# Retention and cross attention of a decoder layer: two stages run one after the other, and the same work issued in one interleaved order

## The chip, the cores and the metric

The kernel runs on one core of a Trainium2 chip. The core has five engines that run their own instruction queues in order: TensorE (PE in the profile; PEld is its weight load), VectorE (DVE), ScalarE (ACT), GpSimd (POOL) and SyncE (SP, which here only issues DMAs). Matmuls write to PSUM, of which there are eight banks of 128 partitions by 512 fp32 values; the other data lie in SBUF. The metric is the time of one execution on the device in microseconds: the median of the runs. All arithmetic here is fp32, except one bf16 matmul that is named below.

## The reference

Input `x` has 16 batches of 128 positions by 512 features; three sublayers follow, each with a residual and a LayerNorm.

1. **Retention**, 16 heads of width 32. For each batch `Q`, `K`, `V`, `G` are projections of `x` (four 512x512 weights). `Q` and `K` are rotated (`x*c + rot(x)*s`, neighbours swapped in pairs). `ret = (Q K^T) * D` with a decay matrix `D`, `Y = ret V`; `Y` is normalised within each head (mean and variance over 32 values), scaled and shifted; the result is `(G * sigmoid(G) * Yn) @ W_O`, added to `x` and normalised.
2. **Cross attention over the feature axis**: the 512 features are the sequence, the 128 positions the channels; 8 heads of width 16. Scores are kept only in a band `|i - j| <= 64`; outside it the softmax weight is zero. Output projection, `relu`, multiplication by `ctx_2048[n]`, a last 128x128 projection, residual, LayerNorm.
3. **A selected feed-forward block**: the 16 best positions of each batch (by a router score) go through an attention block and a gated MLP, and are written back; all other positions only get the last LayerNorm.

## The kernel before

The kernel has three stages, one after the other.

**Retention** (lines 113 to 317) works on `G = 8` groups `g` of two batches. The weights are loaded once; `load(g)` fetches the transposed group `xT` and its rows `xg`. The steps of a group are functions: `rotated` (16 matmuls in the record into one bank; DVE swaps pairs with a stream shuffle and multiplies with the cosine, POOL multiplies the swapped half with the sine and adds), twice for q and twice for k; `values` (once for each batch); `gates` (twice; ACT applies Silu, L206); `retain` (twice: scores of 8 heads into four banks, multiplied by the decay on DVE, L223); `weigh` (twice: times V; ACT writes the square and a copy, L246 and L247); `variance` (a matmul that averages the squares; ACT takes the root, L104, DVE the reciprocal, L105); `normalise` (spreads the factor back over four banks; eight DVE instructions, L269 and L271); `finish` (once for each batch: output projection; DVE adds the row and takes its moments; after both batches, POOL computes the inverse root in one chain, L289 and L290, and DVE writes the normalised rows `xr[n]`, L292). A loop issues the projections of group `g`, the middle steps of group `g - 1` and the `finish` of group `g - 2`, all from one pool of eight PSUM banks and working tiles of two buffers.

**Cross attention** (lines 343 to 574) works on units `m = 0..31`, two for each batch (`n = m // 2`, four heads each). `project` makes q and k of a unit (ACT moves them out of PSUM with the bias, L407), `project_v` the values of a batch. `scores(m, half)` computes half a unit's banded scores in four banks, and DVE adds the band and takes each row's maximum (L435, eight instructions). `lower(m)` transposes the maxima and subtracts them from q (L448). `weights(m, half)` computes the transposed scores: first one bf16 matmul for each of the four banks writes the band itself, an identity times a tile with 0 inside and a huge negative value outside (L457), then the score matmuls add to it (L462), and ACT takes the exponential (L467). `attend(m)` multiplies with the values, `divide(m)` transposes and normalises; `turn(n)` and `project_out(n)` make the output (ACT relu, then POOL times `enc`, L510), and `settle(n)` does the last projection (L516) and the LayerNorm: DVE moments, a chain of four small POOL instructions (L524 to L529), DVE writes `xr[n]` (L530) and the router score (L532), ACT writes the copy `z_plain` (L536), which SP stores.

The order of issue is written out by hand, and each engine runs its part of it in order. For one unit `m` it is: `scores(m+1, 0)`, `project` q, in even units `settle(n-2)`, `weights(m, 0)`, `attend(m-1)`, `project` k, `scores(m+1, 1)`, `divide(m-1)`, in even units `project_v`, `weights(m, 1)`, in odd units `turn(n-1)`, `lower(m+1)`, in odd units `project_out(n-1)`. PSUM is divided into six banks for `scores` and `weights` (a call takes four of them) and two, called misc here, that all other steps take in turn.

Between the two stages all buffers of the first are given back, six 1 MB weight parts of the feed-forward stage are loaded (L331), then the small weights of cross attention (L357).

**The feed-forward stage** follows; the change does not touch its instructions.

## Time and profile before

| what | value |
|---|---|
| median of three runs | 1154.94 us (1154.24 to 1155.27) |
| the profiled execution: its own time | 1148.59 us |
| its span | 1146.8 us |
| first retention matmul | 10.55 us |
| end of the last retention matmul | 353.8 us |
| first cross matmul / first `scores` | 379.33 / 385.90 us |
| last cross work (router score), start of selection | 862.2 us |
| end | 1146.8 us |
| one retention group in the steady part | 41.08 us (start of `normalise`'s matmuls at 70.19 and at 111.27) |
| one cross batch in the steady part | 28.56 us (`project_v` at 452.11 and at 480.67) |

How to read the profile: its first part gives the busy time of each engine. A view in stretches gives, for each stretch of the span, the busy time of PE, PEld, DVE, ACT and POOL with the number of instructions, then the granted TensorE clock (1.00 is full), the share of the DMA engines and their GB/s. The timeline lists instructions in order of time: start, duration, engine, line, what is written from what, and in brackets how long the engine had been idle and who ended that. The groups list, for equal instructions, the busy time, the mean duration in ns, and the idle time before them. Matmul durations in groups overlap each other; what a matmul group costs PE is better read from the distance of the next group's start in the timeline.

### The profile page before, as it was taken

To read this page: it belongs to the slowest core of one execution; us is meant where nothing else is said; L and a number is where in the kernel's file an instruction comes from. 1 tells how busy PE (TensorE), PEld (TensorE's weight loads), DVE (VectorE), ACT (ScalarE), POOL (GpSimd) and SP (SyncE) were. 2 spreads that over 40 slices of the span, in tenths; PEclk is the share of its full clock that TensorE was granted. 3 is DMA by queue.
4 is the path that set the end of the run, shared out by engine and by line. 5 is a ranking of instruction groups with operands and counts; after the bars stand their busy time and mean duration, and the time that the engine had idled before them with its cause. 6 is when DMAs were issued, how large, how long until landed. Compare 5 with 4: busy or idle time off the path is not lost.

```text
span 1146.8 us, 17444 instructions
## 1 busy us (share of the span) xinstructions
PE 990.1 (86%) x6987; PEld 611.4 (53%) x6987; DVE 502.8 (44%) x1778; ACT 338.6 (30%) x660; POOL 170.5 (15%) x189
## 2 busy tenths in 40 slices
PE   6999999999973699999999999999850898788995
PEld 5766767676641355555555555555420574445862
DVE  3344544453552355555555555555424344621102
ACT  0122012112120254444444444444420432411110
POOL 3312312322301001111111111111113141000000
PEclk9999999999996699999999999999965899999998
DMA  9110110010004400000000000000002143004410
GB/s 321 38 37 1 38 37 17 22 37 1 1 1 165 139 1 11 20 19 20 20 20 20 20 20 20 20 20 20 29 9 73 37 139 118 1 1 147 147 37 18
DMA packets 27600, 53.39 MB, mean 47 GB/s; under 512 B 3824, under 2 KB 4608, under 8 KB 27264
## 3 DMA queue, kind: packets, MB, share of 16 engines
q1 hardware_dynamic: 25296, 50.69, 13.3%
q10 hardware_dynamic: 2064, 1.07, 0.4%
q8 instruction: 55, 0.90, 0.3%
q0 software_dynamic: 160, 0.52, 0.1%
q14 instruction: 25, 0.20, 0.1%
HBM read 47.55 MB, written 4.73 MB: 46 GB/s over the span
## 4 chain that ended last, share of the span: by engine, by line
PE 30%; issue 19%; DVE 8%; ACT 7%; POOL 3%; DMA 2%; SPq 1%; POOLq 0%; DVEq 0%
PE xs_ps L427 5%; ACT xp_t L467 5%; PE xt_ps L462 4%; PE qk_ps L702 4%; PE xqk_ps L406 4%; DVE x_masked L435 3%; PE xt_ps L457 3%; PE xav_ps L476 2%; PE xout_ps L507 2%; PE xv_ps L412 1%; DVE bn_st L109 1%; PE xut_ps L489 1%; POOL rs L527 1%; DVE h L518 1%; PE xmx_ps L446 1%
## 5 line engine op out<-in xcount | busy, mean ns | idle before, releaser
L435 DVE CUSTOM_DVE_ANT_0 x_masked<-xs_ps,x_band 128x192 f32<-128x192 f32 (+1 forms) x512 | 164.7, 387 | 142.5 <-PE xs_ps L427 142.1
L467 ACT ACTIVATE xp_t<-xt_ps 128x448 f32<-128x448 f32 x256 | 118.1, 547 | 85.9 <-PE xt_ps L462 85.9
L427 PE MATMUL xs_ps<-xkT,xqT 32*128 32x256 f32 (+1 forms) x1024 | 92.3, 385 | 3.4 <-ACT xp_t L467 1.4
L427 PEld LDWEIGHTS xs_ps<-xkT,xqT 32*128 32x128 f32 x1024 | 58.4, 185 | 51.8 <-issue 36.6
L510 POOL TENSOR_TENSOR xy<-xy,enc 128x512 f32<-128x512 f32 x16 | 20.3, 1267 | 397.9 <-ACT xy L509 397.9
L188 POOL TENSOR_TENSOR swapped<-swapped,consts 128x512 f32<-128x512 f32 x32 | 40.6, 1268 | 206.0 <-DVE swapped L184 205.0
L180 PE MATMUL qT_ps<-xT,w_W_Q 128*128 128x256 f32 x256 | 60.5, 391 | 10.6 <-DMA xT<-in_xT 10.6
L462 PE MATMUL xt_ps<-x_qa,xkT 32*128 32x192 f32 (+1 forms) x1024 | 67.3, 377 | 0.1
L457 PE MATMUL xt_ps<-band_b,ident_b 128*128 128x448 bf16 x256 | 62.2, 356 | 3.7 <-DVE x_mx L435 3.7
L246 ACT ACTIVATE sq<-y_ps 128x512 f32<-128x512 f32 x16 | 9.6, 597 | 174.8 <-PE y_ps L241 174.8
L282 PE MATMUL o_ps<-w_W_O,y 128*128 128x512 f32 x128 | 59.8, 613 | 1.1 <-DVE y L271 1.1
L462 PEld LDWEIGHTS xt_ps<-x_qa,xkT 32*128 32x128 f32 x1024 | 44.0, 186 | 31.2 <-issue 29.8
L406 PE MATMUL xqk_ps<-xp,x_w_q 128*128 128x512 f32 x64 | 37.9, 676 | 25.5 <-DMA x_w_v<-in_w_v 25.5
L180 PE MATMUL kT_ps<-xT,w_W_K 128*128 128x256 f32 x256 | 59.2, 385 | 0.0
L180 PEld LDWEIGHTS qT_ps<-xT,w_W_Q 128*128 128x128 f32 x256 | 49.3, 195 | 18.2 <-DMA xT<-in_xT 10.6
L194 PE MATMUL v_ps<-w_W_V,xT 128*128 128x512 f32 x128 | 58.8, 604 | 0.0
L203 PE MATMUL g_ps<-xT,w_W_G 128*128 128x256 f32 x256 | 58.4, 382 | 0.0
L476 PE MATMUL xav_ps<-xp_t,x_va 128*32 128x192 f32 (+1 forms) x1024 | 55.8, 359 | 0.0
L203 PEld LDWEIGHTS g_ps<-xT,w_W_G 128*128 128x128 f32 x256 | 48.1, 190 | 12.0 <-issue 6.1
L180 PEld LDWEIGHTS kT_ps<-xT,w_W_K 128*128 128x128 f32 x256 | 47.5, 190 | 8.1 <-issue 1.4
L407 ACT ACTIVATE xqT<-xqk_ps,x_b_q 128x512 f32<-128x512 f32 x32 | 22.0, 687 | 89.4 <-PE xqk_ps L406 89.4
L476 PEld LDWEIGHTS xav_ps<-xp_t,x_va 128*32 128x32 f32 x1024 | 30.3, 111 | 25.3 <-issue 12.2
(192 smaller groups left out, 1485.2 us busy)
## 6 DMA issues: line engine op xcount, KB each, us to landing
xT<-in_xT SPq DMA_DIRECT2D x8, 512.0 KB, 3.9
xg<-in_x SPq DMA_DIRECT2D x8, 512.0 KB, 4.8
wq<-in_wq SPq DMA_DIRECT2D x4, 1024.0 KB, 10.8
enc<-in_ctx SPq DMA_DIRECT2D x16, 256.0 KB, 2.8
out<-z_plain SPq DMA_DIRECT2D x16, 256.0 KB, 3.0
wo<-in_wo SPq DMA_DIRECT2D x4, 1024.0 KB, 5.3
w_gate<-in_w_gate SPq DMA_DIRECT2D x4, 1024.0 KB, 5.1
w_up<-in_w_up SPq DMA_DIRECT2D x4, 1024.0 KB, 5.1
```

The source lines that it names most:

```text
L180: nc.tensor.matmul(ps[:, i * GT:(i + 1) * GT], w[wname][:, kc, hg * P:(hg + 1) * P], st["xT"][:, kc, :], start=(kc == 0), stop=(kc == KC - 1))
L194: nc.tensor.matmul(ps, state[g]["xT"][:, kc, b * S:(b + 1) * S], w["W_V"][:, kc, :], start=(kc == 0), stop=(kc == KC - 1))
L203: nc.tensor.matmul(ps[:, i * GT:(i + 1) * GT], w["W_G"][:, kc, hg * P:(hg + 1) * P], state[g]["xT"][:, kc, :], start=(kc == 0), stop=(kc = ...
L282: nc.tensor.matmul(ps, st["y"][:, kc, b * S:(b + 1) * S], w["W_O"][:, kc, :], start=(kc == 0), stop=(kc == KC - 1))
L406: nc.tensor.matmul(ps, w[:, hg * P:(hg + 1) * P], xr[n], start=True, stop=True)
L427: nc.tensor.matmul(ps[j][:, OFF[c]:OFF[c] + LEN[c]], st["qT"][hs, hg, c * P:(c + 1) * P], st["kT"][hs, hg, LO[c]:LO[c] + LEN[c]], start=Tr ...
L435: nc.vector.tensor_tensor_reduce(out=junk[:, 0:LEN[c]], in0=ps[j][:, OFF[c]:OFF[c] + LEN[c]], in1=band[:, SEEN[c]:SEEN[c] + LEN[c]], scale ...
L457: nc.tensor.matmul(ps[j][:, 0:448], ident_b, band_b[:, half, :], start=True, stop=True)
L462: nc.tensor.matmul(ps[j][:, OFF[c]:OFF[c] + LEN[c]], kT[hs, hg, c * P:(c + 1) * P], qa[hs, LO[c]:LO[c] + LEN[c]], start=False, stop=True, ...
L467: nc.scalar.activation(p[:, half, j, :], ps[j][:, 0:448], AF.Exp, scale=XD ** -0.5)
L476: nc.tensor.matmul(ps[32 * j:32 * (j + 1), LO[c]:LO[c] + LEN[c]], va[:, c, hg * 4 + j, :], p[:, c // 2, j, OFF[c]:OFF[c] + LEN[c]], start= ...
L702: nc.tensor.matmul(ps[:, i * R:(i + 1) * R], w[(h0 + i) // 4][:, kc, at:at + P], hT[:, kc, :], start=(kc == 0), stop=(kc == KC - 1))
```

## The change

The two stages become one function `layers` with one order of issue.

- A loop runs `m` from -8 to 35. Each iteration issues the cross attention's steps of unit `m` in the old order, and between them up to four slots of retention steps that `plan(m)` lists. Four iterations (two batches of cross attention) carry one retention group, `g = m // 4 + 2`; `finish` writes rows two batches ahead of their use. Iterations -8 to -3 hold retention alone, 26 to 35 cross attention alone.
- PSUM: all steps share the cross attention's six plus two banks. `retain` and `normalise` take four of the six; `rotated`, `values`, `gates`, `weigh`, `variance` and `finish` take the two misc banks.
- The band: the bf16 matmuls (L457) are gone. `weights` takes the exponential of all columns, and then GpSimd sets what lies outside the band to zero with four `affine_select` instructions for each half unit, each on four heads by 128 (or 64) columns of the weights.
- The gate: ACT's Silu becomes `tanh(g/2)`, and DVE computes `(tanh + 1) * g`; the factor one half is put into `gn_weight` and `gn_bias`, which DVE multiplies by 0.5 at the start.
- Rows: `load` fetches the rows straight into `xr`, `finish` works on them in place, and each batch has its own inverse root on POOL.
- Working tiles of retention have one buffer instead of two in most places; the weights' tile `xp_t` has three half-unit buffers.
- Small weights of cross attention are loaded during retention; `decay` is loaded before `W_G`. Centring `W_V` on DVE is issued at the end of iteration -8. The six feed-forward weight parts are loaded at the end of iteration 25, when the retention buffers are given back.

```diff
+    def layers(left: ExitStack, right: ExitStack):
         G = B // GB
+        wp = right.enter_context(tc.tile_pool(name="ret_w", bufs=1, side="right"))
+        wk = right.enter_context(tc.tile_pool(name="ret_wk", bufs=1, side="right"))
+        xw = left.enter_context(tc.tile_pool(name="x_w", bufs=1))
+        xk = left.enter_context(tc.tile_pool(name="x_wk", bufs=2))
+        sp = left.enter_context(tc.tile_pool(name="scores_ps", bufs=6, space=PSUM))
+        mp = left.enter_context(tc.tile_pool(name="misc_ps", bufs=2, space=PSUM))
+
+        def score_bank(name):
+            return sp.tile([P, 512], F32, tag="score", name=name)
+
+        def misc_bank(name):
+            return mp.tile([P, 512], F32, tag="misc", name=name)
...
-            xT = wk.tile([P, KC, GT], F32, name="xT")
+            xT = wk.tile([P, KC, GT], F32, name="xT", bufs=2)
             nc.sync.dma_start(out=xT, in_=t["xT"][:, g])
-            xg = wk.tile([P, GB, D], F32, name="xg", bufs=4)
-            nc.sync.dma_start(
-                out=xg, in_=t["x"][g * GB:(g + 1) * GB].rearrange("b s d -> s b d"))
-            state[g] = dict(
-                xT=xT, xg=xg,
-                qT=wk.tile([P, 4, GB, S], F32, name="qT"),
-                kT=wk.tile([P, 4, GB, S], F32, name="kT"),
-                v=wk.tile([P, GB, D], F32, name="v"),
-                gate=wk.tile([P, 4, GT], F32, name="gate"))
+            for i in range(GB):
+                nc.sync.dma_start(out=xr[g * GB + i], in_=t["x"][g * GB + i])
+            state[g] = dict(xT=xT)
...
+            nc.vector.tensor_scalar_mul(v, v, 0.5)
...
+        def centre():
+
+            wv = w["W_V"].rearrange("p k (h d) -> p (k h) d", d=HD)
+            wmean = wp.tile([P, KC * NH], F32, name="w_mean")
+            nc.vector.tensor_reduce(wmean, wv, AX.X, ALU.add)
+            nc.vector.tensor_scalar_mul(wmean, wmean, 1.0 / HD)
+            nc.vector.tensor_tensor(wv, wv, bc(wmean, 2, HD), ALU.subtract)
...
-            nc.scalar.activation(state[g]["gate"][:, 2 * hp:2 * hp + 2, :],
-                                 ps.rearrange("p (i n) -> p i n", i=2), AF.Silu)
+            if hp == 0:
+                state[g]["gate"] = wk.tile([P, 4, GT], F32, name="gate")
+            pv = ps.rearrange("p (i n) -> p i n", i=2)
+            gt = state[g]["gate"][:, 2 * hp:2 * hp + 2, :]
+            nc.scalar.activation(gt, pv, AF.Tanh, scale=0.5)
+            nc.vector.scalar_tensor_tensor(gt, gt, 1.0, pv, ALU.add, ALU.mult)
...
+            sc = [score_bank(f"ret_ps{j}") for j in range(4)]
...
+            ps = [score_bank(f"spread_ps{hg}") for hg in range(4)]
...
-            if b == 0:
-                st["h"] = wk.tile([P, GB, D], F32, name="h1")
-                st["mv"] = small.tile([P, GB, 2], F32, name="mv1")
-            h, mv = st["h"], st["mv"]
-            ps = bank("o_ps")
+            row = xr[g * GB + b]
+            ps = misc_bank("o_ps")
             for kc in range(KC):
                 nc.tensor.matmul(ps, st["y"][:, kc, b * S:(b + 1) * S], w["W_O"][:, kc, :],
                                  start=(kc == 0), stop=(kc == KC - 1))
-            nc.vector.tensor_tensor(h[:, b, :], ps, st["xg"][:, b, :], ALU.add)
-            moments(mv[:, b, :], h[:, b, :])
-            if b < GB - 1:
-                return
-            rs = small.tile([P, GB], F32, name="rs1")
-            nc.gpsimd.tensor_scalar(rs, mv[:, :, 1], 1.0, EPS, ALU.mult, ALU.add)
-            nc.gpsimd.tensor_tensor(rs, rs, power, ALU.pow)
...
+            nc.vector.tensor_tensor(row, ps, row, ALU.add)
+            mv = small.tile([P, 2], F32, name="mv1")
+            moments(mv, row)
+            rs = small.tile([P, 1], F32, name="rs1")
+            nc.gpsimd.tensor_scalar(rs, mv[:, 1:2], 1.0, EPS, ALU.mult, ALU.add)
+            nc.gpsimd.tensor_tensor(rs, rs, power[:, 0:1], ALU.pow)
+            nc.vector.tensor_scalar(row, row, mv[:, 0:1], rs, ALU.subtract, ALU.mult)
+            if b == GB - 1:
+                state.pop(g)
...
             ps = [score_bank(f"xt_ps{j}") for j in range(4)]
-            for j in range(4):
-                nc.tensor.matmul(ps[j][:, 0:448], ident_b, band_b[:, half, :],
-                                 start=True, stop=True)
             for c in (2 * half, 2 * half + 1):
                 for j in range(4):
                     hs = slice(32 * j, 32 * (j + 1))
                     nc.tensor.matmul(ps[j][:, OFF[c]:OFF[c] + LEN[c]],
-                                     kT[hs, hg, c * P:(c + 1) * P],
+                                     kT[hs, c * P:(c + 1) * P],
                                      qa[hs, LO[c]:LO[c] + LEN[c]],
-                                     start=False, stop=True, skip_group_check=True)
+                                     start=True, stop=True)
             for j in range(4):
-                nc.scalar.activation(p[:, half, j, :], ps[j][:, 0:448], AF.Exp,
-                                     scale=XD ** -0.5)
+                nc.scalar.activation(p[:, j, :], ps[j][:, 0:448], AF.Exp, scale=XD ** -0.5)
+
+            for c in (2 * half, 2 * half + 1):
+                for sign, a, b in ((1, SEEN[c], P), (-1, P, SEEN[c] + LEN[c])):
+                    v = p[:, :, OFF[c] + a - SEEN[c]:OFF[c] + b - SEEN[c]]
+                    nc.gpsimd.affine_select(
+                        out=v, in_=v, pattern=[[0, 4], [sign, b - a]],
+                        base=a if sign == 1 else P - a, channel_multiplier=-sign,
+                        compare_op=ALU.is_ge, fill=0.0)
...
+        def ret(*units):
+            for f, g, *args in units:
+                if 0 <= g < G:
+                    f(g, *args)
+
+        def plan(m):
+
+            k, it = divmod(m, 4)
+            g = k + 2
+            if it == 0:
+                return ([(load, g + 1), (rotated, g, "q", "W_Q", 0, 0)], [(normalise, g - 1)],
+                        [(rotated, g, "k", "W_K", 1, 0)], [])
+            if it == 1:
+                return ([(finish, g - 1, 0)], [(retain, g, 0)],
+                        [(values, g, 0)], [(finish, g - 1, 1)])
+            if it == 2:
+                return ([(values, g, 1)], [(weigh, g, 0)],
+                        [(rotated, g, "q", "W_Q", 0, 1)], [(rotated, g, "k", "W_K", 1, 1)])
+            return ([(gates, g, 0)], [(retain, g, 1)],
+                    [(gates, g, 1)], [(weigh, g, 1), (variance, g)])
+
+        for m in range(-8, M + 4):
+            n, odd = divmod(m, 2)
+            nxt = 0 <= n + 1 < B
+            a, b, c, d = plan(m)
+            guarded(scores, m + 1, 0)
+            ret(*a)
+            if m == -6:
+                prepare()
+            if nxt:
+                project(n + 1, w_q, b_q, "q", odd)
+            if not odd and 0 <= n - 2 < B:
+                settle(n - 2)
+            guarded(weights, m, 0)
+            ret(*b)
+            guarded(attend, m - 1)
+            if nxt:
+                project(n + 1, w_k, b_k, "k", odd)
+            guarded(scores, m + 1, 1)
+            ret(*c)
+            if m == -8:
+                centre()
+            guarded(divide, m - 1)
+            if not odd and nxt:
+                project_v(n + 1)
+            guarded(weights, m, 1)
+            if odd and 0 <= n - 1 < B:
+                turn(n - 1)
+            ret(*d)
+            guarded(lower, m + 1)
+            if odd and 0 <= n - 1 < B:
+                project_out(n - 1)
+            if odd and 0 <= n < B:
+                encoder(n)
+            if m == 4 * (G - 1) - 3:
+                right.close()
+                start_ff()
+
+    first = {}
+
+    def start_ff():
+        nonlocal wff
+        wff = ctx.enter_context(tc.tile_pool(name="ff_w", bufs=7, side="right"))
+        first["wq"] = [kc_part("wq", i) for i in range(4)]
+        first["wk"] = [kc_part("wk", i) for i in range(2)]
+
+    with ExitStack() as left, ExitStack() as right, tc.manual_schedule():
+        layers(left, right)
```

## The prediction

> **What bounds the kernel now.** I read the page first, then stretches, then the timeline of one cross batch. Each stretch line gives the window, then PE, PEld, DVE, ACT and POOL busy, the granted clock, the DMA share and GB/s.
>
> ```profile
> span 1146.8 us, 17444 instructions
> 116.00:154.00 38.00, 38.00 (x260) 25.17 (x259) 16.69 (x31) 6.84 (x11) 11.02 (x10) 1.00 0.09 28
> 358.00:380.00 22.00, 0.67 (x1) 0.50 (x2) 0.00 (x0) 0.00 (x0) 2.74 (x6) 0.50 0.93 319
> 485.70:514.30 28.60, 26.51 (x249) 14.57 (x249) 15.70 (x77) 13.54 (x26) 2.88 (x5) 1.00 0.07 19
> ...
> 379.33 2.05 PE L406 MATMUL xqk_ps<-xp,x_w_q 128*128 128x512 f32 x2 [25.54 <-DMA x_w_v<-in_w_v]
> ```
>
> Retention is PE alone, with no idle time. Between the stages PE waits 25.54 us for weights. In cross attention every engine has idle time: there a chain sets the pace, and the next view shows which.
>
> ```profile
> 561.27 0.70 POOL L527 TENSOR_TENSOR rs<-rs,power 128x2 f32<-128x2 f32 x1
> 562.07 0.53 POOL L529 TENSOR_SCALAR shift<-mv,rs 128x1 f32<-128x1 f32 x1
> 562.63 0.81 ACT L536 ACTIVATE z_plain<-h,shift,rs 128x512 f32<-128x512 f32 x1 [4.40 <-POOL shift L529]
> 563.10 2.28 PE L427 MATMUL xs_ps<-xkT,xqT 32*128 32x256 f32 x16
> 563.35 1.82 ACT L467 ACTIVATE xp_t<-xt_ps 128x448 f32<-128x448 f32 x4
> ...
> 836.61 1.61 PE L507 MATMUL xout_ps<-xoT,x_w_outT 128*128 128x512 f32 x2 [1.91 <-ACT xoT L502]
> 840.35 2.07 PE L516 MATMUL xct_ps<-xy,x_w_ct 128*128 128x512 f32 x2 [2.12 <-POOL xy L510]
> ```
>
> The reader is to see two things. ACT works in order: `z_plain` waits for `settle`'s POOL chain, and the exponentials of `weights`, ready 2.8 us before, stand behind it; `scores` takes 2.28 instead of 1.0 us, because its banks wait for them. And after waits of about 2 us a matmul pair takes 2.07 us against 1.13 in the steady part (557.61): TensorE runs at half speed.
>
> **How I cost the new order.** I walk one period of four iterations, instruction by instruction, through the four in-order queues as the built kernel has them, with start-to-start distances of this profile. PE: `scores`, `weights` 0.97, `project` 1.05, `attend` 1.65, one `rotated` 3.46, `values` 3.43, `gates` 3.46, one `finish` 3.52, `retain` 1.11, `weigh` 1.01, `variance` 0.57, the four-transpose steps 0.59. DVE: eight maxima 2.55, a `rotated` 1.3, `normalise` 3.7, four decays 2.5. ACT: four exponentials 1.85. The same walk through the old even unit puts `attend`, `divide` and `project_v` within 0.3 us of the trace.
>
> PE's sum without the band is 18.4, 22.0, 22.2 and 20.1 us for iterations 4k to 4k+3: 82.7, and 83.7 with the 1.0 by which a measured group (41.08) exceeds its parts (40.1). Before, the same work takes 41.08 + 2 x 28.56 = 98.2. Waits that the walk finds:
> - 4k+3, 3.7 us: `retain` waits 1.0 for banks that exponentials hold; `turn` 0.75 for `divide`, behind the gate's new multiply on DVE; `variance` 1.0 for the square, behind four exponentials on ACT; `project_out` 1.1 for the misc bank that the root (table load 1.28, root 0.47) holds.
> - 4k, 7.4 us. From its first `scores`: `rotated` runs 1.4 to 4.9 (behind `lower`'s bank, as DVE subtracts only after the reciprocal of 1.75), DVE empties its bank by 6.5, `settle` runs 6.5 to 7.6, `weights` to 8.5, and its exponentials could begin at 8.7. But DVE's moments end at 9.3, POOL's chain at 11.1, `z_plain` at 12.0, and a table load (1.28, since the root came before) at 13.3: only then do they begin. `normalise` does two of its banks by 8.9 and needs the first exponential for another, at 13.75: PE idles 4.9. `attend` starts at 14.5, `scores` ends at 18.2, `rotated` k at 21.6, its bank is empty at 23.2, so `project_v` waits 1.0; the unit ends at 25.8. Other places 1.5.
> - 4k+1, 1.4 us: `retain` 0.9 for banks, the rest small.
> - 4k+2, 6.0 us: `values` waits 1.3 for `lower`'s bank, since DVE's subtraction stands behind `finish`, which waits for POOL; `project` k waits 3.9 for `weigh`'s bank, whose two reads on ACT stand behind the exponentials, behind `z_plain`; `project_v` 0.9.
>
> Sum 83.7 + 18.5 = 102.2. The waits of 4.9 and 3.9 exceed those after which the trace shows half speed; an episode lasts 3.3 us there (823.3 to 826.6) and so costs half, 1.7. I add two, and half of a third for the three waits near 1 us in 4k+3 (before 823.3, two of 1.2 within 8 us were enough): 4.2. The period is 106.4, between 102.2 (no episode) and 107.3 (three).
>
> [...]
>
> **Parts that the period holds, or that other work hides.**
> - Band: 256 bf16 matmuls, four in 0.85 us: 54 us of PE go, already left out. In cross attention alone the chain stays: by the walk an even unit takes 13.55 and an odd one 14.05, against 14.28 each.
> - Selections: 256, seven sizes of 512 elements for each unit in sum. No row has the operation. Bounds for one of 512: a memset 523 ns (L386), a two-input add 1385 (L189). I take 0.84, from the one-input copy (L650: 284 ns for 128) and the one-element memset (about 100): 100 + 512 x 1.44. A half unit takes 2.9; POOL is then busy about 41 of 106 us. At 0.52 the end is 2 us earlier; at 1.39, 13 later (`finish`'s POOL step stands behind them on POOL, as does `xy`, 1.1 a period and 6 at the end). A gain beyond that is excluded: they replace nothing on POOL.
> - Tanh: 16 DVE multiplies of 0.75 (as L518), and 8 Silu loads of 1.28 go; the loads left, for the root and back, are counted above.
> - Rows in place, an inverse root for each batch: one more POOL pair of 0.9 per group, inside the waits counted.
> - DMAs: `xT` of the next group stands on SP behind `enc`, which waits for POOL's `xy` early in iteration 4k; it is read a period later. The 25.54 us wait goes, since SP issues the small weights during retention, behind `W_O`. Six weight parts, 9.3 us of SP (357.76 to 367.08), come at iteration 25; behind them stand `z_plain` stores whose buffer is next written a batch later. The 105 us of cross units after it cover them; without that cover they cost their 20 us again. DVE's two multiplies by 0.5 wait for small loads that landed by 9.3, before its first eviction at 16.3: nothing.
>
> **Sum to the end of cross attention (862.2 before).** Iterations -8 to -1 hold two groups with little to fill in: the walk gives 103.7 (PE idles 3.5 for POOL's rotation at 19.5, 2.0 for the centring of `W_V`, one half-clock episode). Then 6 x 106.4 = 638.4, less 15.6 in the first period (no `settle`, `attend`, `turn` yet), 39 for iterations 24 and 25, and 105 for the rest (106.8 before from 755.4; 4 saved, one episode back). 103.7 + 638.4 - 15.6 + 39 + 105 = 870.5: 8.3 us later. The rest, 284.6, is unchanged. The profiled execution took 1148.59 us, 6.4 below the median of 1154.94; 8.3 on top gives 1156.9 and, at the median, **1163**. Less than 0.2% (2.3 us) is no change that this kernel's runs can tell.
>
> **The rivals.** Break-even is at a period of (862.2 - 232.1) / 6 = 105.0.
> - *Faster: the clock stays full.* If TensorE holds speed through the two long waits the period is 102.2 and the end 25 us earlier, 1138. For it: cross units keep clock 1.00 with waits of 1.2 each. Against: 836 to 842. It decides when fewer than two episodes fall in a period. Chance 0.27.
> - *The `z_plain` wait does not bite*, so PE stays near its sum: period 93 to 84, 1083 to 1029. Against: the built order has `z_plain`, the table load, then the exponentials. 0.06.
> - *Slow selections.* At 2 us each, `finish` and the last units lose 35 us: 1200; from 3.0 POOL's own sum (28 selections and 18 us of other work) passes the walked period. 0.17.
> - That the interleaving is not built as written is excluded by the built order.
>
> [...]
>
> **How the numbers follow.** The forecast holds 0.50 (1150 to 1178; slower 0.43, same 0.05, faster 0.02). The full-clock case gives faster 0.26, same 0.01; the third rival 0.06 faster; slow selections 0.17 slower. Together: faster 0.34, same 0.06, slower 0.60. The range 1120 to 1205 leaves out the third rival with the edge of the second's side, and the selections above 2 us.
>
> **What would show it.** After: `normalise`'s and `project` k's idle time put down to ACT's exponentials; clock below 1.00 between 110 and 730; a four-iteration period near 106; selections near 0.84; no wait for the small weights; `scoreT` near 870. A period below 105.0, or selections above 1.4, makes the forecast wrong.

## The result, and the profile after

The changed kernel takes 1171.9 us (median of four, 1170.2 to 1172.3) against 1154.6 us before: a ratio of 1.0157, with a 95% interval of 1.0126 to 1.0188. The sign of the forecast (1163, +0.7%) was right, its size less than half of what was measured. The profiled execution took 1170.15 us, 1.7 below its median; that of before stood 6.0 below the median of 1154.6. On the two profiles' own scale the change costs 21.6 us, where the working had 8.3.

First the page of the changed kernel: the span, two of the costliest groups, and the granted clock in tenths over 40 slices of the span.

```profile
span 1168.4 us, 17280 instructions
...
PEclk9999999899899989998998999888865799999998
...
L397 DVE CUSTOM_DVE_ANT_0 x_masked<-xs_ps,x_band 128x192 f32<-128x192 f32 (+1 forms) x512 | 199.7, 390 | 136.7 <-PE xs_ps L389 98.8
L433 POOL TENSOR_SCALAR_AFFINE_SELECT xp_t<-xp_t 128x512 f32<-128x512 f32 (+1 forms) x256 | 141.0, 588 | 268.2 <-ACT xp_t L428 268.2
```

The clock falls below 0.9 in five slices of the merged stage (those that begin at 204, 292, 409, 526 and 613 us), as foretold, and in every slice from 730 to 935 us, from just before cross attention runs alone until into the selection. Then the stretches of one period of four iterations (the first four lines, 4k to 4k+3, each from its first `scores` to the next) and of an odd and an even unit of cross attention alone. Columns: window, length, then PE, PEld, DVE, ACT and POOL busy with their counts, the granted clock, DMA share, GB/s.

```profile
407.82:436.78 28.96, 22.81 (x159) 14.28 (x158) 17.37 (x56) 7.68 (x13) 10.32 (x13) 0.88 0.16 56
436.78:460.63 23.85, 23.04 (x172) 12.35 (x171) 13.92 (x46) 8.18 (x17) 7.38 (x15) 1.00 0.00 1
460.63:489.46 28.83, 23.96 (x192) 15.91 (x191) 13.50 (x47) 9.08 (x17) 10.35 (x17) 0.94 0.06 20
489.46:513.46 24.00, 21.58 (x220) 14.65 (x219) 13.39 (x44) 10.16 (x18) 7.01 (x11) 1.00 0.00 1
786.78:800.62 13.84, 12.48 (x116) 6.92 (x115) 8.35 (x36) 7.36 (x15) 5.92 (x11) 1.00 0.35 129
800.62:817.72 17.10, 14.92 (x120) 9.23 (x119) 9.76 (x40) 6.10 (x12) 5.69 (x11) 0.80 0.10 32
```

The period is 105.6 us here (105.8 on average from one `variance` to the next, 298.03 to 721.13 in four), where 106.4 was forecast. Iterations 4k and 4k+2, which hold a `settle`, are 5 us longer than the others and are the ones with a clock below 1.00. In cross attention alone an odd unit takes 13.84, near its forecast; an even one takes 17.10 at a clock of 0.80, where 13.55 was forecast, and that is where the forecast fails.

The timeline of iteration 4k (start, length, engine, line, operation; in brackets the idle time before it and who ended it) shows the mechanism in the merged stage:

```profile
415.98 0.60 PE L330 MATMUL spread_ps<-gn_rs,spread 32*128 32x256 f32 x4
...
418.91 0.81 ACT L506 ACTIVATE z_plain<-h,shift,rs 128x512 f32<-128x512 f32 x1 [4.82 <-POOL shift L499]
...
419.74 1.28 ACT L428 ACT_TABLE_LOAD   x1
...
420.01 0.69 PE L330 MATMUL spread_ps<-gn_rs,spread 32*128 32x256 f32 x2 [3.43 <-DVE y L334]
...
421.03 1.85 ACT L428 ACTIVATE xp_t<-xt_ps 128x448 f32<-128x448 f32 x4
...
421.63 1.22 PE L330 MATMUL spread_ps<-gn_rs,spread 32*128 32x256 f32 x2 [0.93 <-ACT xp_t L428]
422.78 3.21 PE L444 MATMUL xav_ps<-xp_t,x_va 128*32 128x192 f32 x32
...
425.92 2.08 PE L362 MATMUL xqk_ps<-xp,x_w_k 128*128 128x512 f32 x2
```

`z_plain` waits for POOL, and the table load (ACT_TABLE_LOAD, 1.28 us; the trace has seven at this line, each between a root and the next exponentials) and the exponentials stand behind it. `normalise` waits 3.43 and 0.93 us, and then `attend` takes 3.21 us (1.72 at full speed) and `project` k 2.08 (1.13). Summed over the kernel, these waits (engine and line, who ended them, us, times, longest) are new or have grown:

```profile
PE spread_ps L330 <- DVE y L334: 21.1, 6, 3.9
PE xqk_ps L362 <- ACT y L312: 19.6, 6, 3.9
...
PE xs_ps L389 <- ACT xp_t L428: 7.6, 3, 3.1
```

The third line belongs to the even units at the end: three waits of 2 to 3 us for exponentials, where the sum had units without them. What makes them longer than before can be seen when the maxima of `scores` are laid side by side. Before, on DVE, in cross attention:

```profile
557.09 0.35 DVE L435 CUSTOM_DVE_ANT_0 x_masked<-xs_ps,x_band 128x192 f32<-128x192 f32 x1
557.37 0.08 DVE L435 DVE_READ_ACCUMULATOR2_ANT x_mx<- 128x1 f32 x1
557.37 0.42 DVE L435 CUSTOM_DVE_ANT_0 x_masked<-xs_ps,x_band 128x256 f32<-128x256 f32 x1
557.71 0.08 DVE L435 DVE_READ_ACCUMULATOR2_ANT x_mx<- 128x1 f32 x1
557.71 0.35 DVE L435 CUSTOM_DVE_ANT_0 x_masked<-xs_ps,x_band 128x192 f32<-128x192 f32 x1
```

After, in the even unit of the table above:

```profile
801.68 0.36 DVE L397 CUSTOM_DVE_ANT_0 x_masked<-xs_ps,x_band 128x192 f32<-128x192 f32 x1 [1.31 <-PE xs_ps L389]
801.96 0.08 DVE L397 DVE_READ_ACCUMULATOR2_ANT x_mx<- 128x1 f32 x1
802.08 0.42 DVE L397 CUSTOM_DVE_ANT_0 x_masked<-xs_ps,x_band 128x256 f32<-128x256 f32 x1
802.43 0.08 DVE L397 DVE_READ_ACCUMULATOR2_ANT x_mx<- 128x1 f32 x1
802.65 0.36 DVE L397 CUSTOM_DVE_ANT_0 x_masked<-xs_ps,x_band 128x192 f32<-128x192 f32 x1
...
805.35 0.75 DVE L488 SCALAR_TENSOR_TENSOR h<-xct_ps,x_b_ct,xp 128x512 f32<-128x512 f32 x1
```

One maximum takes as long as before (0.35 and 0.42), and the group's mean is 390 ns against 387. But the distance to the next start was 0.28 and 0.34 us, and is now 0.40 and 0.57: eight take 801.68 to 805.35, 3.67 us, against 2.50 (556.46 to 558.96 before). The reason is a part of the change that the text ahead of the prediction does not name: their scratch tile `x_masked` has one buffer where it had two.

```diff
-                    junk = wk.tile([P, KW], F32, name="x_masked")
+                    junk = xk.tile([P, D], F32, name="x_masked", bufs=1)
```

With two buffers the next maximum starts 0.07 us before the recorded end of the one before it; with one it starts 0.04 to 0.15 us after it. `settle`'s `h` stands behind all eight on DVE, and `z_plain` and the exponentials behind that.

Milestones of the profile beside the forecast: first iteration of the merged stage 108.3 (forecast 103.7); 24 iterations later 724.9, so 616.7 for them (622.8); iterations 24 and 25 42.3 (39); from there to the transpose of the router scores (`scoreT`), with which the selection begins, at 884.8, 117.5 (105); the rest 283.6 (284.6). The misses are +4.6, -6.1, +3.3, +12.5 and -1.0 us, in sum 13.3. The largest by far is the stretch of cross attention alone; the other four nearly cancel.

### The profile page after: what moved, and what is told of

The parts are those of the page before. It is cut to its first block, busy times and chain, and to the rows that moved or that the text cites. A ratio compares the mean times of both kernels' runs of the same rounds, so it can differ in the third digit from the quotient of the medians.

```text
span 1168.4 us, 17280 instructions
## 1 busy us (share of the span) xinstructions
PE 973.6 (83%) x6731; PEld 615.6 (53%) x6731; DVE 560.6 (48%) x1791; ACT 340.4 (29%) x659; POOL 314.9 (27%) x461
## 3 DMA queue, kind: packets, MB, share of 16 engines
q10 hardware_dynamic: 2064, 1.07, 0.4%
## 4 chain that ended last, share of the span: by engine, by line
PE 52%; issue 20%; DVE 14%; ACT 7%; POOL 4%; DMA 2%; DVEq 0%; POOLq 0%; ACTq 0%; SPq 0%
DVE x_masked L397 5%; PE xs_ps L389 5%; PE xt_ps L423 5%; PE xqk_ps L362 5%; PE g_ps L263 5%; PE o_ps L344 5%; PE xav_ps L444 4%; PE qk_ps L703 4%; PE q_ps L237 4%; PE v_ps L254 4%; ACT xp_t L428 3%; PE k_ps L237 3%; PE ret_ps L283 2%; PE xv_ps L376 2%; DVE bn_st L109 1%
## 5 line engine op out<-in xcount | busy, mean ns | idle before, releaser
L397 DVE CUSTOM_DVE_ANT_0 x_masked<-xs_ps,x_band 128x192 f32<-128x192 f32 (+1 forms) x512 | 199.7, 390 | 136.7 <-PE xs_ps L389 98.8
L433 POOL TENSOR_SCALAR_AFFINE_SELECT xp_t<-xp_t 128x512 f32<-128x512 f32 (+1 forms) x256 | 141.0, 588 | 268.2 <-ACT xp_t L428 268.2
L389 PE MATMUL xs_ps<-x_kT,x_qT 32*128 32x256 f32 (+1 forms) x1024 | 80.4, 401 | 7.6 <-ACT xp_t L428 7.6
L389 PEld LDWEIGHTS xs_ps<-x_kT,x_qT 32*128 32x128 f32 x1024 | 52.4, 197 | 54.4 <-issue 32.8
L423 PE MATMUL xt_ps<-x_qa,x_kT 32*128 32x256 f32 (+1 forms) x1024 | 76.4, 394 | 1.7 <-DVE x_qa L410 0.9
L237 PE MATMUL q_ps<-xT,w_W_Q 128*128 128x256 f32 x256 | 67.1, 420 | 11.0 <-DMA xT<-in_xT 10.7
L423 PEld LDWEIGHTS xt_ps<-x_qa,x_kT 32*128 32x128 f32 x1024 | 49.2, 194 | 34.5 <-issue 20.0
L237 PEld LDWEIGHTS q_ps<-xT,w_W_Q 128*128 128x128 f32 x256 | 52.8, 212 | 24.8 <-DMA xT<-in_xT 10.7
L237 PE MATMUL k_ps<-xT,w_W_K 128*128 128x256 f32 x256 | 59.4, 385 | 0.6 <-DVE ret_qT L244 0.6
L362 PE MATMUL xqk_ps<-xp,x_w_k 128*128 128x512 f32 x64 | 42.7, 753 | 19.9 <-ACT y L312 19.6
L237 PEld LDWEIGHTS k_ps<-xT,w_W_K 128*128 128x128 f32 x256 | 47.4, 190 | 9.9 <-issue 2.4
L444 PEld LDWEIGHTS xav_ps<-xp_t,x_va 128*32 128x32 f32 x1024 | 34.1, 124 | 28.6 <-issue 14.7
```

The source lines that it names most:

```text
L237: nc.tensor.matmul(ps[:, i * GT:(i + 1) * GT], w[wname][:, kc, hg * P:(hg + 1) * P], st["xT"][:, kc, :], start=(kc == 0), stop=(kc == KC - 1))
L362: nc.tensor.matmul(ps, wt[:, hg * P:(hg + 1) * P], xr[n], start=True, stop=True)
L389: nc.tensor.matmul(ps[j][:, OFF[c]:OFF[c] + LEN[c]], qT[hs, c * P:(c + 1) * P], kT[hs, LO[c]:LO[c] + LEN[c]], start=True, stop=True)
L397: nc.vector.tensor_tensor_reduce(out=junk[:, 0:LEN[c]], in0=ps[j][:, OFF[c]:OFF[c] + LEN[c]], in1=band[:, SEEN[c]:SEEN[c] + LEN[c]], scale ...
L423: nc.tensor.matmul(ps[j][:, OFF[c]:OFF[c] + LEN[c]], kT[hs, c * P:(c + 1) * P], qa[hs, LO[c]:LO[c] + LEN[c]], start=True, stop=True)
L433: nc.gpsimd.affine_select(out=v, in_=v, pattern=[[0, 4], [sign, b - a]], base=a if sign == 1 else P - a, channel_multiplier=-sign, compare ...
```

## Experiments

Each kernel was compared with the kernel before on the same chip, where it took 1149.5 to 1152.1 us; ratios are to that, with their 95% interval. The changed kernel's 1.0157 is 1168 us on this scale.

### z_plain behind the exponentials

```diff
             guarded(weights, m, 0)
             ret(*b)
+            if late:
+                plain(*late.pop())
```

`plain` holds `z_plain` and its store, taken out of `settle`.

> Only ACT's z_plain and its store move, behind the four exponentials of the same half unit and the retention step after them. Theory (ACT's queue: z_plain, waiting for POOL's chain, holds the exponentials, and TensorE runs at half speed after the wait): in iteration 4k the third normalise matmul still waits for DVE, which waits for POOL's root, so only the wait for the exponentials and part of the attend delay go, 1.9 us; in 4k+2 project k's wait of 3.8 us shrinks to about 0.6 and the half speed after it goes, 4.8 us. Period 105.7 to about 99, even cross-only units 17.1 to about 14.2, whole kernel 1172 to about 1126. Rival (the waits are set by the two misc banks, or by POOL, and z_plain only fills time that is lost anyway): within 5 us of 1172.

Measured: 1129.4 us, ratio 0.9817 [0.9790, 0.9845]; 39 us below the changed kernel, where 46 were expected. The period is 98.8 (expected 99). In iteration 4k one `normalise` matmul now waits for the exponentials behind their table load, and the next for DVE, which stands behind POOL's root:

```profile
507.29 0.69 PE L330 MATMUL spread_ps<-gn_rs,spread 32*128 32x256 f32 x2 [1.55 <-ACT xp_t L428]
509.17 1.21 PE L330 MATMUL spread_ps<-gn_rs,spread 32*128 32x256 f32 x2 [1.18 <-DVE y L334]
```

`project` k in 4k+2 waits 0.45 us in place of 3.82 (552 to 559 us of this run). So the wait named in the prediction is real and is worth 39 us; the rival that it only filled lost time falls.

### The whole end of settle later

```diff
             guarded(scores, m + 1, 1)
+            if late:
+                plain(*late.pop())
             ret(*c)
```

Here `plain` holds DVE's normalised row and score, `z_plain` and the store.

> The end of settle (DVE's two steps that need POOL's root, ACT's z_plain, the store) moves behind the second half of scores. Theory (settle's chain stands in ACT's and DVE's queues ahead of ready work): normalise's wait of 3.4 us and the half speed after it go as well, period 105.7 to about 94, even cross-only units 17.1 to 13.6 to 14.2 with a granted clock of 1.00, whole kernel 1172 to about 1095. Rival (misc banks or POOL hold the period): 1160 to 1172. If z_plain alone was the cause, this run and the one with only z_plain moved come out within 5 us of each other; if DVE's share counts, this one is 20 us or more faster.

Measured: 1118.7 us, ratio 0.9736 [0.9704, 0.9769]; its profiled execution, at 1107, lies 11 below that. Better than `z_plain` alone by 11 us, not by the 30 expected. `normalise`'s wait for DVE went (the one for the exponentials stayed, up to 1.6 us), but DVE's two steps now stood ahead of the eviction of `rotated`, and `project_v` waited 2.3 us for it twice a period, once behind each `rotated`; the first of the two in sum (us, times, longest):

```profile
PE xv_ps L376 <- DVE ret_qT L244: 12.3, 6, 2.3
```

A step that leaves one queue position needs a place where nothing is waiting behind it; this place was wrong for DVE.

### The selections alone, in the kernel before

```diff
-                nc.tensor.matmul(ps[j][:, 0:448], ident_b, band_b[:, half, :],
-                                 start=True, stop=True)
...
+            for c in (2 * half, 2 * half + 1):
+                for sign, a, b in ((1, SEEN[c], P), (-1, P, SEEN[c] + LEN[c])):
+                    v = p[:, half, :, OFF[c] + a - SEEN[c]:OFF[c] + b - SEEN[c]]
+                    nc.gpsimd.affine_select(
+                        out=v, in_=v, pattern=[[0, 4], [sign, b - a]],
+                        base=a if sign == 1 else P - a, channel_multiplier=-sign,
+                        compare_op=ALU.is_ge, fill=0.0)
```

> The kernel before with one part of the change: POOL's selections in place of the band matmuls. Theory (the band matmuls lay beside the wait for z_plain and kept TensorE's waits short; without them the even unit's wait grows past 2 us and half speed follows): even units 14.28 to about 17.1, odd 14.28 to about 13.9, so 2.4 us more for each of 16 batches, 1154.6 to about 1190 although 54 us of TensorE's work go. Rival (the units only get shorter, as the walk without a clock term had it, 13.55 and 14.05): about 1140. Second rival (POOL's selections late): odd units too above 14.3, attend waits for POOL.

Measured: 1127.8 us, ratio 0.9807 [0.9779, 0.9835]: 22 us faster. My theory, that the lost band matmuls had been the even unit's cover, is refuted; the rival's 1140 is nearer. Three units of this run, even, odd, even:

```profile
682.67:696.22 13.55, 12.23 (x120) 6.91 (x119) 8.54 (x40) 6.08 (x12) 5.62 (x11) 1.00 0.12 41
696.22:709.26 13.04, 12.05 (x116) 6.80 (x115) 7.21 (x36) 7.48 (x16) 5.97 (x11) 1.00 0.01 2
709.26:724.19 14.93, 13.61 (x120) 8.29 (x119) 8.53 (x40) 6.07 (x12) 5.62 (x11) 0.89 0.12 36
```

With the selections an even unit takes 13.55, exactly as walked, and 14.93 in every second batch, at a clock of 0.89; an odd one 13.04, 1.0 less than walked. So the 17.10 of the changed kernel does not come from the selections or from the missing matmuls. This run led to the comparison of the maxima.

### Idle matmuls in the waits

```diff
+                if hg == 2 and g > 0:
+                    keep_busy(ps[1], 8)
...
+            if 0 <= m < 24 and m % 4 == 2:
+                keep_busy(score_bank("busy"), 8)
...
+            if 26 <= m < M and not odd:
+                keep_busy(score_bank("busy"), 5)
```

The first stands in `normalise`, the second ahead of `project` k, the third ahead of the second half of `scores`; `keep_busy` issues so many matmuls of 128x256 into a part of a bank that nothing reads.

> The changed kernel with idle matmuls added, whose results nothing reads, where TensorE waits: eight of 128x256 between normalise's second and third matmul, eight ahead of project k in iterations 4k+2, five ahead of the second half of scores in the even units from 26 on. They move no other instruction and fill about the waits (3.4, 3.8 and 2.1 us). Theory (half speed after the waits is a cost by itself): the waits stay, what follows them runs at full speed, 3.1 us in 4k and 1.6 in 4k+2 go, even cross-only units 17.1 to about 14, whole kernel 1172 to about 1136, with a granted clock of 1.00 from 110 to 840 us. Rival (the slow stretches are not the clock but work that waits for banks): 1172 to 1176.

Measured: 1148.7 us, ratio 0.9990 [0.9975, 1.0005]; 19 us below the changed kernel, by work that computes nothing, where 36 were expected. In the merged stage it did what was expected, at a clock of 1.00 from 100 to 730 us:

```profile
411.86 3.72 PE L417 MATMUL spread_ps<-consts 128*128 128x256 f32 x16
415.51 0.69 PE L332 MATMUL spread_ps<-gn_rs,spread 32*128 32x256 f32 x2
416.98 0.69 PE L332 MATMUL spread_ps<-gn_rs,spread 32*128 32x256 f32 x2 [0.78 <-ACT xp_t L435]
417.61 1.72 PE L451 MATMUL xav_ps<-xp_t,x_va 128*32 128x192 f32 x32
419.25 1.13 PE L364 MATMUL xqk_ps<-xp,x_w_k 128*128 128x512 f32 x2
```

The waits are filled, not shortened, and `attend` and `project` k take their full-speed times. The period is 101.1 (399.36 to 702.61 in three) against 105.8: half speed costs 4.7 us a period in the merged stage, beside the 4.2 of the prediction. At the end it gained less: the stretch from iteration 26 to `scoreT` takes 115.1 (749.35 to 864.46) against 117.5. The first two even units fall from 19.5 and 17.1 to 17.6 and 15.9, so half speed was worth 1.9 and at least 1.2 us there; most of what is left above 13.55 is the waits themselves, which the idle matmuls fill and do not shorten. The odd units in turn rose to 14.8 and 14.9: after waits of 0.28 and 1.07 us for DVE (776 to 779 us of this run) `project_out` took 2.06 us (2.02 in the second), 1.13 at full speed, at their ends.

### Two scratch buffers for the maxima

```diff
-                    junk = xk.tile([P, D], F32, name="x_masked", bufs=1)
+                    junk = xk.tile([P, 256], F32, name="x_masked", bufs=2)
...
-            junk = xk.tile([P, D], F32, name="x_masked", bufs=1)
+            junk = xk.tile([P, D], F32, name="xoT", bufs=1)
```

The second pair is the scratch of the router score.

> The changed kernel with two scratch buffers for the maxima in place of one (256 columns each, the same memory; the router score takes another scratch tile), as the kernel before has. Theory (with one buffer each maximum waits for the one before to be written out; eight take 3.67 us in the changed kernel against 2.55 before, and settle stands behind them on DVE): eight maxima take 2.55 again, h and z_plain come 1.1 us earlier, the wait for the exponentials in the even cross-only units falls from 2.1 to about 0.9 and the half speed after it goes: even units 17.1 to about 14.0, odd 13.9 to about 13.0; in the merged stage DVE sets the pace only in places, period 105.7 to about 104. Whole kernel 1172 to about 1148. Rival (the half speed comes from the missing band matmuls alone): even units stay at 16 to 17, whole kernel 1165 to 1172.

Measured: 1154.9 us, ratio 1.0050 [1.0026, 1.0074]; about 12 us below the changed kernel, of the 24 expected. Most of it lies at the end:

```profile
790.97:805.67 14.70, 13.39 (x119) 8.12 (x118) 8.53 (x40) 6.06 (x12) 5.67 (x11) 0.88 0.11 37
805.67:818.87 13.20, 12.15 (x116) 6.89 (x115) 7.21 (x36) 7.60 (x16) 5.91 (x11) 1.00 0.00 1
```

Even units fall from 17.10 to 14.70, odd ones from 14.02 to 13.20, and the stretch from iteration 26 to `scoreT` from 117.5 to 107.6 us (760.94 to 868.57): 9.9 of the 12.5 that the prediction missed there. Of the 2.6 left, the two even units are 3.4 and 1.2 above the walk (16.9 and 14.7) and the two odd ones 1.8 below it. Iterations 24 and 25, which hold little retention, take 38.7 (722.24 to 760.94) in place of 42.3; forecast were 39. The period stays 105.7: in the merged stage DVE has room for the slower maxima.

### One scratch buffer, in the kernel before

```diff
-                    junk = wk.tile([P, KW], F32, name="x_masked")
+                    junk = wk.tile([P, KW], F32, name="x_masked", bufs=1)
```

> The kernel before with one scratch buffer for the maxima in place of two, and nothing else. Theory (one buffer costs 1.1 us for eight maxima on DVE, and settle's chain is behind them): the even unit's wait grows from 1.2 to about 2.3 us and half speed follows, even units 14.28 to about 17, odd 14.28 to about 14.8, 3 us or more a batch and 16 batches: 1154.6 to about 1195. Rival (DVE has room, maxima off the chain): within 5 us of 1154.6.

Measured: 1199.5 us, ratio 1.0425 [1.0407, 1.0442]. One argument, in a kernel that is otherwise the one before, costs 49 us. Three units, even, odd, even:

```profile
701.56:719.68 18.12, 16.70 (x128) 9.70 (x127) 9.77 (x40) 6.07 (x12) 2.88 (x5) 0.81 0.11 31
719.68:734.56 14.88, 12.97 (x123) 6.93 (x123) 8.36 (x36) 7.49 (x16) 0.00 (x0) 1.00 0.00 1
734.56:751.42 16.86, 15.11 (x127) 8.86 (x126) 9.78 (x40) 6.07 (x12) 2.88 (x5) 0.90 0.10 32
```

Even units go from 14.28 to 16.9 and 18.1, at clocks of 0.90 and 0.81, odd ones to 14.88. It is the same fault as in the even units of the changed kernel, and nothing else of the change is in this run.

### Small loads first, in the kernel before

```diff
-    wq = [kc_part("wq", i) for i in range(4)]
-    wk_ = [kc_part("wk", i) for i in range(2)]
...
         nc.sync.dma_start(out=band, in_=t["band"][:, 1])
+        wq.extend(kc_part("wq", i) for i in range(4))
+        wk_.extend(kc_part("wk", i) for i in range(2))
```

> The kernel before with the cross stage's small loads issued ahead of the six weight parts of the last stage. It prices one term of the prediction alone: the 25.54 us in which TensorE waits for the small weights. Theory (the loads stand behind the parts on SP): the wait falls to 5 to 8 us, 1154.6 to about 1136. Rival (the memory comes free late, or the parts are then missed at the other end): within 5 us of 1154.6.

Measured: 1133.1 us, ratio 0.9844 [0.9815, 0.9873]. The wait for the small weights is 7.11 us in place of 25.54, and TensorE waits for no weight part in the last stage:

```profile
361.00 2.04 PE L408 MATMUL xqk_ps<-xp,x_w_q 128*128 128x512 f32 x2 [7.11 <-DMA x_w_q<-in_w_q]
```

### The merged order with its three faults mended

The changed kernel with two scratch buffers, `z_plain` behind the second half of `scores`, and DVE's end of `settle` behind `divide`:

```diff
             guarded(scores, m + 1, 1)
+            if late:
+                plain(*late[0])
             ret(*c)
...
             guarded(divide, m - 1)
+            if late:
+                standard(*late.pop())
```

> The changed kernel with two scratch buffers for the maxima, z_plain and its store behind the second half of scores, and DVE's end of settle behind divide. Theory (chain in ACT's and DVE's queues, the scratch buffer and the clock together make what the change lost): period 105.7 to about 95, cross-only units about 13.2, granted clock 1.00 to the last two units, whole kernel 1172 to about 1083, below both kernels. Rival (the gains overlap, as each removes the same wait): no better than the run with settle moved alone, 1119.

Measured: 1091.7 us, ratio 0.9496 [0.9478, 0.9514]; 27 us better than the run with `settle` moved to the wrong place for DVE; this difference holds the scratch buffer too. The period is 95.8 (573.66 to 669.49) where 95 was expected, and the last units take 24.8 a batch, where two of 13.2 were. The end, 9 us above the 1083 expected, was not traced further.

### The same gains without the common order

The kernel before with the selections and with the small loads first (the two diffs above, and the band's two tiles left out); then the same with `settle`'s end moved as in the best merged kernel:

```diff
                 guarded(scores, m + 1, 1)
+                if late:
+                    plain(*late[0])
                 guarded(divide, m - 1)
+                if late:
+                    standard(*late.pop())
```

> The kernel before, retention and cross attention one after the other, with two things that the change brought: POOL's selections in place of the band matmuls, and the small loads ahead of the weight parts. Theory (the gain of the change lies in these two, 22 and 17 us in the runs that did one alone, and they add, since they lie in different stretches; the common order itself gives nothing): 1150 to about 1111, 40 us or more below the changed kernel with its scratch buffer mended (1155). Rival (the common order is worth something by itself): no faster than 1155 less the half-speed costs, that is 1125 or more.

Measured: 1110.1 us, ratio 0.9635 [0.9610, 0.9660]. The two single gains, 22 and 17 us, add up to the 41 found.

> The run seq with settle's end moved as in the best merged kernel (z_plain behind the second half of scores, DVE's end behind divide). Theory (cross attention alone then runs at TensorE's own pace, 24.8 us a batch as the last units of the best merged kernel do, and retention at 41.1 us a group; 41.1 + 2 x 24.8 = 90.8 is less than the best merged period of 95.8): 16 batches of 28.56 become 24.9, so 1150 - 17 - 59 = about 1074, below the best merged kernel (1092). Rival (in this order POOL's or DVE's share holds the units at 26.5): about 1098, above it.

Measured: 1072.3 us, ratio 0.9305 [0.9281, 0.9330]. A batch of cross attention, both units, at full clock:

```profile
542.16:566.90 24.74, 23.37 (x233) 13.48 (x232) 15.48 (x76) 13.77 (x26) 11.07 (x22) 1.00 0.07 23
```

So retention and cross attention one after the other, with the change's two useful parts, beat the changed kernel by 58 us (1168 against 1110), and the best version of this beats the merged one with the same mends by 22 us (by the ratios). The common order had not paid for anything up to here.

### One more misc bank in the merged order

```diff
-        sp = left.enter_context(tc.tile_pool(name="scores_ps", bufs=6, space=PSUM))
-        mp = left.enter_context(tc.tile_pool(name="misc_ps", bufs=2, space=PSUM))
+        sp = left.enter_context(tc.tile_pool(name="scores_ps", bufs=5, space=PSUM))
+        mp = left.enter_context(tc.tile_pool(name="misc_ps", bufs=3, space=PSUM))
```

> The best merged kernel (two scratch buffers, settle's end moved) with three misc banks and five score banks in place of two and six. Theory (what is left of the period, 95.8 us against 83.7 of matmuls, is waits for the two misc banks: 1.05 twice for project_v, 1.05 for project_out, 0.7 for settle's product, 0.45 for project k): about 4 us a period go, 1092 to about 1068. Rival (the score banks are as short: with five, scores and weights wait for exponentials everywhere, the 32 units too): 1100 or more.

Measured: 1068.5 us, ratio 0.9281 [0.9244, 0.9319], the expected time to 0.5 us. The period falls from 95.8 to 90.3 (189.55 to 640.79 in five). The waits of `project_v`, 1.05 us twice a period, are no longer among the larger ones; what is left are the table load ahead of the exponentials, and the square:

```profile
PE spread_ps L330 <- ACT xp_t L428: 10.4, 7, 1.6
...
PE var_ps L318 <- ACT sq L311: 6.7, 8, 1.0
```

Its interval overlaps that of the best sequential kernel: the runs do not tell them apart. The sequential kernel was not tried with three misc banks, so which order is better with the same banks stays open. Both beat the kernel before by 7%.

### The gate through tanh

The best sequential kernel with one more part of the change:

```diff
-            nc.scalar.activation(state[g]["gate"][:, 2 * hp:2 * hp + 2, :],
-                                 ps.rearrange("p (i n) -> p i n", i=2), AF.Silu)
+            pv = ps.rearrange("p (i n) -> p i n", i=2)
+            gt = state[g]["gate"][:, 2 * hp:2 * hp + 2, :]
+            nc.scalar.activation(gt, pv, AF.Tanh, scale=0.5)
+            nc.vector.scalar_tensor_tensor(gt, gt, 1.0, pv, ALU.add, ALU.mult)
```

> The run seq_late with one more part of the change, the gate through tanh with DVE's multiply. Theory (retention alone is TensorE without a wait, so neither the table loads nor the multiplies matter there): within 3 us of seq_late's 1072. Rival (DVE's 16 multiplies of 0.75 us delay the evictions): 1075 to 1084; or the loads mattered: 1062 to 1068.

Measured: 1071.8 us, ratio 0.9300 [0.9273, 0.9327]: the same as without it. In retention alone TensorE has no idle time that table loads could have cost (in the kernel before it is busy 38.00 us of the 38 from 116 to 154 us). What tanh is worth in the merged order, where a load stands ahead of the exponentials anyway, was not tried.

## Why the prediction was right, and where it was wrong

**The period: right, by its own terms.** The walk had 106.4 for a period; 105.8 was measured. It had 7.4 and 6.0 us of waits in iterations 4k and 4k+2 and 3.7 and 1.4 in the others, and the trace has the long iterations in those places. Single waits: `normalise` 4.9 forecast, 3.43 + 0.93 measured; `project` k 3.9 against 3.82; `project_out` 1.1 against 1.05; `variance` 1.0 against 0.75; `project_v` 1.0 against 1.05; `values` 1.3 in 4k+2 did not come. (Two of the prediction's lists add up to a little more than the totals beside them, 3.85 for 3.7 and 6.1 for 6.0; that would be 1.5 us over six periods.) One detail was off: the first of `normalise`'s two waits is ended by DVE, which stands behind POOL's root, and not by the exponentials, so that moving `z_plain` alone removed less there. Half speed: 4.2 a period forecast, 4.7 by the run with idle matmuls.

**The clock after waits: as the row had it, and sooner.** The prediction went by the row that shows half speed after waits of about 2 us. In the changed kernel an even unit at the end fell to half speed after a wait of 2.08 us (`project_v` at 813.45 took 1.91 us, against 1.16 in the kernel before at 566.29), and in the run with `z_plain` moved `attend` took 3.21 us (1.72 at full speed) after waits of 1.55 and 1.18. The last section has shorter waits before half speed.

**Selections: right in kind, priced too high.** Taken at 0.84 us for 512 elements; 141.0 us over the kernel, 0.64 for 512 and 0.42 for 256. The rival of slow selections, at 2 us each, falls. Their use in the kernel before is worth 22 us.

**Small loads, loads of weights at iteration 25, the last stage: right.** No wait for the small weights shows, and the last stage takes 283.6 against 284.6.

**The prologue: 103.7 forecast, 108.3 measured.** TensorE waited 3.51 and 2.60 us, near the walk (3.5 and 2.0). The two `values` after it took 9.3 us, where two of 3.43 and a half-clock episode of 1.7 were counted, and a wait of 1.41 us for POOL's rotation (at 69.11) is not in the walk. These make 2.8 of the 4.6; the rest was not traced.

**The merged iterations: 622.8 forecast, 616.7 measured.** Most of these 6.1 us lies in the first period: from one `variance` to the next it takes 85.5 us (106.83 to 192.30), 20.3 less than the later ones, where 15.6 were taken off. That this makes up for the prologue and for iterations 24 and 25 is luck.

**The step that failed: "105 for the rest ... 4 saved, one episode back".** From iteration 26 to `scoreT` it took 117.5 us: 12.5 us more, nearly the whole miss of 13.3. The term stood on even units of 13.55 and odd ones of 14.05, which were walked with "eight maxima 2.55", taken from the trace of before. The change makes these eight take 3.67, with one buffer for `x_masked`. The term "eight maxima" was mis-sized by 1.1 us, and the even units were walked with no clock episode, although the prediction had noted itself that two waits of 1.2 us within 8 us had been enough for one. The first two even units took 19.5 and 17.1. Giving the buffer back brings the stretch to 107.6, and iterations 24 and 25 to 38.7, beside their 39; taking it away from the kernel before costs that one 49 us. With two buffers and the selections an even unit takes the walked 13.55 when the clock holds and 14.7 to 14.9 when it does not. The first even unit exceeds it more (16.9 with two buffers): there TensorE waits 1.06 us more, for DVE behind the last `finish` (see the last section).

**The rivals.** *The clock stays full* fell as a forecast, but its price was right: the run with idle matmuls, which keeps it full, has a period of 101.1, and 102.2 was written. *The `z_plain` wait does not bite* fell: moving it alone is worth 39 us. *Slow selections* fell by the group above.

**Where the expected gain went.** What took 98.2 us before became 82.7 us of matmuls a period. The runs put the loss in places: 39 to `z_plain` alone, 12 to the scratch buffer, and, in the kernel with both mended, 25 to the third misc bank (by the ratios). They overlap, so they are not to be added; and the half speed, 4.7 a period, lies partly inside the first. With all of them mended, the third misc bank among them, the common order comes to the same time as the old order with the selections, the small loads and `settle`'s end moved. What the change gains, it gains by the selections and by the small loads.

## What to carry to other kernels

When a row's duration is carried over to changed code, check its start-to-start distance and whether a buffer count on its operands has changed: the mean of one maximum was the same to 1% (390 against 387 ns), and a scratch output with one buffer still made eight of them take nearly half as long again (3.67 us against 2.50). In an in-order queue, look for the step that waits for a long chain and needs nothing itself (here `z_plain`), and put it behind the work that others wait for; place each engine's share of it apart. Before merging two stages to fill idle time, mend the idle time where it is: here that gave as much, without merging, as the best merged kernel reached.

## What the runs showed of the hardware

The same wait was followed by half speed or by full speed. In the kernel before with selections, the second half of `scores` waits 0.88 to 0.97 us in the eleven even units at 446 to 555 and 636 to 773 us. `project_v`, two steps later, takes 1.16 us, full speed, in the first two of them, and then half speed (1.91 or 1.92) and full speed in turn:

```profile
691.19 1.45 PE L427 MATMUL xs_ps<-xkT,xqT 32*128 32x256 f32 x12 [0.89 <-ACT xp_t L464]
692.97 0.66 PE L493 MATMUL xut_ps<-consts,xu 128*128 128x128 f32 x4 [0.33 <-ACT xu L485]
693.57 1.16 PE L412 MATMUL xv_ps<-x_w_v,xp 128*128 128x128 f32 x8
...
717.78 1.45 PE L427 MATMUL xs_ps<-xkT,xqT 32*128 32x256 f32 x12 [0.89 <-ACT xp_t L464]
719.56 1.09 PE L493 MATMUL xut_ps<-consts,xu 128*128 128x128 f32 x4 [0.33 <-ACT xu L485]
720.44 1.91 PE L412 MATMUL xv_ps<-x_w_v,xp 128*128 128x128 f32 x8
```

The length of these waits does not decide it alone: 0.89 and 0.33 us within 2 us stand ahead of half speed at 720.44 and ahead of full speed at 693.57. In this run the pattern repeats after two batches, 54.6 us (691.19 to 745.75). What else decides it was not shown.

A selection on POOL, with its condition on the index, took 0.64 us for 128x512 in fp32 in the changed kernel (mean of 192), half of what a two-input multiply of that shape took there (`xy`, 1.27).

One DVE instruction took three times as long beside a POOL instruction. In the changed kernel DVE's last step of `finish` (L352) takes 0.55 us in ten of 16 cases, in which POOL does nothing at that time, and 1.62 or 1.63 in the other six, all of which lie beside POOL's `xy` (L480, 1.26 us):

```profile
754.36 0.55 DVE L352 TENSOR_SCALAR xp<-xp,mv,rs 128x512 f32<-128x512 f32 x1 [0.96 <-POOL rs L351]
768.06 1.62 DVE L352 TENSOR_SCALAR xp<-xp,mv,rs 128x512 f32<-128x512 f32 x1 [0.96 <-POOL rs L351]
```

In the kernel before, the same step (L292) took 0.54 to 0.55 us in all 16 cases. The walk had no term for this. The maxima of the kernel before were not slowed: they ran beside `xy` at their usual 0.36 and 0.42 us (556.46 to 557.37). In the first even unit of cross attention alone, `settle`'s product waits 1.07 us for the subtraction (L410) that stands behind this step.
